# A graph-network kernel whose start is reordered: first adjacency on ScalarE's queue, late weights fetched and folded beside it

## The chip, the cores and the metric

The kernel runs on one core of one Trainium2 chip. The metric is device time in microseconds for one execution, from the first to the last instruction. Of the engines, TensorE (PE) multiplies, VectorE (DVE), ScalarE (ACT) and GpSimd (POOL) do the elementwise work, and SyncE (SP) only issues transfers. A transfer is issued in the program of one of these engines and then carried by 16 DMA engines that all queues share.

## The reference, cut to what matters

There are 16 graphs of 1024 nodes with 128 features, and each graph has a full 1024 x 1024 adjacency in float32. Two layers follow each other, each with a residual and a normalization.

```python
# layer 0: one aggregation
degree = adj.sum(axis=-1)[:, :, None]
sum_neighbors = einsum('bid,bij->bjd', x, adj) / degree
x = layernorm(x + relu(concat([x, sum_neighbors]) @ W.T + b))

# layer 1: four inner layers, which use the adjacency both ways
def _layer(nodes, adj, ws, bs, wd, bd, wn, bn, wu, bu):
    src_agg = einsum('bjv,bij->biv', nodes @ ws + bs, l2norm(adj, 2))
    dst_agg = einsum('bjv,bji->biv', nodes @ wd + bd, l2norm(adj, 1))
    upd = concat([src_agg, nodes @ wn + bn, dst_agg])
    return tanh(upd @ wu + bu)
# inner layers three and four take the outputs of earlier ones beside their own input
x = layernorm(x + layer4(layer3(layer2(layer1(x)))))
```

The product `(nodes @ ws) @ wu` is one product with folded weights `ws @ wu`. The kernel folds the weights of each inner layer once, on the chip, and keeps the folded ones in DRAM for the later graphs.

## The kernel before: the parts that the change touches

The first graph is handled apart, ahead of the loop over graphs. Transfers are issued first. The pieces of the first adjacency are split between SyncE's and GpSimd's queue; all weights and the reloaded rows of the adjacency follow on SyncE's.

```python
    def load_pair(q, pair, groups):
        h, k = pair
        for g in groups:
            q.dma_start(a[g * C:(g + 1) * C, h * BPH + k:h * BPH + k + 2], av[h][g, :, k:k + 2])
    ...
    nc.sync.dma_start(w0n, w0)
    shares = ((nc.sync, range(G // 2)), (nc.gpsimd, range(G // 2, G)))
    for h in (1, 0):
        for q, groups in shares:
            load_nodes(q, h, groups)
    make_identity(nc, ident)
    for pair in PAIRS:
        for q, groups in shares:
            load_pair(q, pair, groups)
    ...
    for l, q in enumerate((None, 2, 3, None)):
        fetched.append(fetch_weights(raw, l, nc.sync, None if l else wm))
        if q is not None:
            rows[q] = load_rows(0, q, [places[q]])
    for q in (0, 1):
        rows[q] = load_rows(0, q, [places[q]])
```

A pair is two of the eight row blocks of the adjacency. It comes in four pieces of 32 partitions and 256 KB. `fetch_weights` issues eight transfers for a layer: `ws`, `wd`, `wn`, `wu` and four biases. `load_rows` issues eight for a quarter of the adjacency's rows.

The fold of a layer has two parts. `small` takes one of two PSUM buffers in turn.

```python
    def fold_begin(l, fetched, copy=nc.scalar.copy, later=False):
        wr, wur, bc, wm, wTs = fetched
        for c in range(CHUNKS[l]):                     # CHUNKS = [1, 1, 2, 3]
            pt = small(f"wtr{l}_{c}", [BPH, P])
            for k in range(3):
                nc.tensor.transpose(pt[:, k], wr[:, k, c], ident)
            copy(wTs[c], pt[:, :3])
        pm = small(f"bm{l}", [HW])
        ...                                            # bias products into pm
        def biases():
            nc.scalar.copy(wm[:, 0], pm[:, :2 * P])
            nc.scalar.activation(bout[l], pm[:, 2 * P:2 * P + 1], AF.Identity, bias=bc[:, 3:4])
        return biases if later else biases()

    def fold_end(l, fetched):
        for c in range(CHUNKS[l]):
            pm = small(f"wm{l}_{c}", [HW])
            for k in range(3):
                nc.tensor.matmul(pm[:, k * P:(k + 1) * P], wTs[c][:, k], wur[:, PART[k]], ...)
            nc.scalar.copy(wm[:, 1 + c], pm[:, :2 * P])
            nc.scalar.copy(wown[l][:, c], pm[:, 2 * P:3 * P])
        nc.sync.dma_start(wsave[l], wm[:, :CHUNKS[l] + 1])
```

Then the first aggregation gathers the blocks pair by pair, while ScalarE squares them and VectorE sums their rows.

```python
    for h in (1, 0):
        to_xT(h)
        with_x(h)
        weights_of_x(h)
    for pair in PAIRS[:2]:
        squares_of(*pair)          # ScalarE squares, VectorE row sums
        gathers_of(*pair)          # TensorE, four products of 128 x 512
    ...
    degree_row(1)
    squares_of(*PAIRS[2])
    gathers_of(*PAIRS[2])
    ...                            # the fourth pair, the fold of layers one and two, the normalization
```

In the first inner layer the folds of layers three and four stand between the 34 products (`hooks` are run ahead of a product with that number):

```python
            hooks = {4: lambda *_: inverses(0, st0, NB), 5: folded(2, fold_begin), 6: rows0, 7: cinv0,
                     8: folded(2, fold_end), 9: lambda *_: fold_and_scale(3, 0), 11: second0, 12: folded(3, fold_end),
                     14: lambda *_: scale_rows(rows[1], 1, rinv), 18: first0, 26: sums0}
            plain_layer(b, 0, feats, t, a, at, f1, "acc", hooks)
```

The order of the instructions on TensorE, VectorE, ScalarE and GpSimd is the order in which they are written; that of SyncE's is left to the scheduler.

Of the kernel before, what the change touches and what calls it, by code (L numbers as in the profile page):

```python
# [14 lines left out]
P = 128  # L15
NL = 4
CHUNKS = [1, 1, 2, 3]
G = 4
# [5 lines left out]
def adj_resnorm_kernel(ctx: ExitStack, tc: tile.TileContext, x, adj, w0, b0, layers, out):  # L24
# [33 lines left out]
    nc = tc.nc  # L58
    B, N, D = x.shape
    NB = N // P  # L60
    HW = 512
# [9 lines left out]
    def blocks(ap):  # L71

        return ap.rearrange("p (k g c) -> p g k c", g=G, c=C)

    def nodes(ap):

        return ap.rearrange("p (g k c) -> p g k c", g=G, c=C)

    def half(h):
        return slice(h * HW, (h + 1) * HW)  # L80
# [12 lines left out]
    ident = const.tile([P, P], F32, name="ident")  # L93
    fold = const.tile([P, P], F32, name="fold")
    group = const.tile([P, G], F32, name="group")
    mhalf = const.tile([P, K], F32, name="mhalf")
    w0T = const.tile([P, 2, P], F32, name="w0T")
# [27 lines left out]
    def fetch_weights(raw, l, q, wm=None):  # L125
        ws, bs, wd, bd, wn, bn, wu, bu = layers[l]
        nch = CHUNKS[l]
        flat = raw.take(max(3 * nch * P, (nch + 1) * 2 * P))
        wr = flat[:, :3 * nch * P].rearrange("p (k c v) -> p k c v", k=3, c=nch)
        for k, w in enumerate((ws, wd, wn)):  # L130
            q.dma_start(wr[:, k], w.rearrange("(c p) v -> p c v", p=P))
        wur = raw.take(3 * P).rearrange("p (k v) -> p k v", k=3)
        q.dma_start(wur, wu.rearrange("(c p) v -> p c v", p=P))
        bc = raw.take(4)
        for k, v in enumerate((bs, bd, bn, bu)):
            q.dma_start(bc[:, k:k + 1], v.rearrange("(p o) -> p o", o=1))
        if wm is None:
            wm = flat[:, :(nch + 1) * 2 * P].rearrange("p (c v) -> p c v", c=nch + 1)
        return wr, wur, bc, wm, [raw.take(3 * P).rearrange("p (k v) -> p k v", k=3) for _ in range(nch)]
# [37 lines left out]
    def small(name, shape=(K,)):  # L177
        return ps_s.tile([P, *shape], F32, tag="small", name=name)
# [362 lines left out]
    def load_rows(b, q, st, queue=nc.sync):  # L541


        v = adj[b, q * QB * C:(q + 1) * QB * C].rearrange("(k r) (h g j) -> h g r k j", r=C, h=NH, g=G)
        n = QB // len(st)
        for i, piece in enumerate(st):
            for g in range(G):
                for h in range(NH):
                    queue.dma_start(piece[g * C:(g + 1) * C, :, h * P:(h + 1) * P], v[h, g, :, i * n:(i + 1) * n])  # L549
        return st  # L550

    def scale_rows(st, q, rinv):
        n = QB // len(st)
        for k in range(QB):
            row = st[k // n][:, k % n]
            nc.scalar.activation(row, row, AF.Copy, scale=rinv[:, q * QB + k:q * QB + k + 1])
# [248 lines left out]
    PAIRS = [(h, k) for h in (1, 0) for k in range(0, BPH, 2)]  # L805
# [5 lines that stand above are left out]
# [3 lines left out]
            q.dma_start(xn[g * C:(g + 1) * C, h * BPH:(h + 1) * BPH], xv[h][g])  # L814

    nc.sync.dma_start(w0n, w0)
    shares = ((nc.sync, range(G // 2)), (nc.gpsimd, range(G // 2, G)))
    for h in (1, 0):
        for q, groups in shares:
            load_nodes(q, h, groups)  # L820
    make_identity(nc, ident)
    for pair in PAIRS:
        for q, groups in shares:
            load_pair(q, pair, groups)
    nc.sync.dma_start(b0c, b0.rearrange("(p o) -> p o", o=1))
    raw = Raw()
    wm = message_tile("wm1_0")
    Q = combined(0, "Q")
    places = {q: Q[i].rearrange("p k (u c) -> p (k u) c", u=2) for q, i in ((2, 2), (3, 3), (0, 4))}
    places[1] = one.tile([P, 2 * NJ, HW // 2], F32, tag="T2", name="rows1_0")  # L830
    rows, fetched = {}, []
    for l, q in enumerate((None, 2, 3, None)):
        fetched.append(fetch_weights(raw, l, nc.sync, None if l else wm))
        if q is not None:
            rows[q] = load_rows(0, q, [places[q]])
    for q in (0, 1):
        rows[q] = load_rows(0, q, [places[q]])

    nc.vector.memset(mhalf, -0.5)
    nc.vector.reduce_sum(fold[:, :C], ident.rearrange("p (g c) -> p c g", g=G), axis=AX.X)  # L840
    for g in range(1, G):
        nc.vector.tensor_copy(fold[:, g * C:(g + 1) * C], fold[:, :C])
# [6 lines left out]
    def to_xT(h):  # L849
        pt = small(f"xtr0_{h}", [HW])  # L850
        for q in range(BPH):
            nc.tensor.transpose(pt[:, q * P:(q + 1) * P], xn[:, h * BPH + q], ident)
        nc.scalar.copy(nodes(xT[:, half(h)]), blocks(pt))

    pt = small("w0tr", [HW])
    for k in range(2):
        nc.tensor.transpose(pt[:, k * P:(k + 1) * P], w0n[:, k * P:(k + 1) * P], ident)
    nc.scalar.copy(w0T.rearrange("p k v -> p (k v)"), pt[:, :2 * P])

    sq = []  # L860
    for p in (3, 4):
# [73 lines left out]
    for h in (1, 0):  # L935
        to_xT(h)
        with_x(h)
        weights_of_x(h)
    for pair in PAIRS[:2]:
        squares_of(*pair)  # L940
        gathers_of(*pair)
    nc.vector.tensor_add(sq[6], sq[6], sq[7])
# [52 lines left out]
    for b in range(B):  # L995
# [8 lines left out]
        if b == 0:  # L1004
            def row_factors0():
                nonlocal rinv
                rinv = gather_inverses(0, row_inverses(0, inv))
                column_sums(0, st0)
                for q in (2, 3):
                    scale_rows(rows[q], q, rinv)  # L1010

            t = messages(b, 0, feats, wm, {0: lambda: to_x1(0), 2: row_factors0}, with_sums=False)
            cinv = {}

            def columns0(rows, h, engine=nc.vector):
                scale_columns(a, cinv[0], rows, half(h), engine)

            def rows0(destination, finish):
                for q in (2, 3):
                    transpose_rows(rows[q], q, at)  # L1020

            def cinv0(destination, finish):
                cinv[0] = factor_rows_now(0, 1, inv, "cinv")

            def second0(destination, finish):
                columns0(range(NJ, NB), 1)
                destination(1, cinv[0])
                columns0(range(NJ), 1)

            def fold_and_scale(l, q):  # L1030
                fold_begin(l, fetched[l])
                scale_rows(rows[q], q, rinv)

            def first0(destination, finish):
                columns0(range(NJ, NB), 0, nc.gpsimd)
                columns0(range(2), 0, nc.gpsimd)
                for q in (0, 1):
                    transpose_rows(rows[q], q, at)
                destination(0, cinv[0])
                columns0(range(2, NJ), 0)  # L1040

            def sums0(destination, finish):
                combine_1(y)
                finish(1)
                combine(2, y, T)
                combine_1(yt)
                combine(3, y, T)

            def folded(l, part):
                return lambda *_: part(l, fetched[l])  # L1050

            hooks = {4: lambda *_: inverses(0, st0, NB), 5: folded(2, fold_begin), 6: rows0, 7: cinv0,
                     8: folded(2, fold_end), 9: lambda *_: fold_and_scale(3, 0), 11: second0, 12: folded(3, fold_end),
                     14: lambda *_: scale_rows(rows[1], 1, rinv), 18: first0, 26: sums0}
            T = combined(0, "T")
            plain_layer(b, 0, feats, t, a, at, f1, "acc", hooks)
            wm = message_weights(b, 1)
            a2 = load(n)
            xs2 = load_spread(n)
        else:  # L1060
            w = {}
            if nxt:
                w["a"] = load(n)
                st = begin_sums(n)
            t = messages(b, 0, feats, wm)
            wm = message_weights(b, 1)
            Q = combined(b, "Q")

            def rows3():
                for q in (1, 0):  # L1070
                    transpose_rows(rows[q], q, at)

            def sums1(w=w, st=st):
                if nxt:
                    for i in range(2):
                        squares_of_row(n, w["a"], st, i)
                    for i in range(2):
                        degree_of(w["a"], st, i)

            def first_addition(st=st):  # L1080
                if nxt:
                    add_squares(n, st, 1)

            hooks = {0: rows3, 3: lambda: combine(4, y, T), 5: lambda: combine_1(yt), 7: lambda: combine(2, yt, Q),
                     9: lambda: combine(3, yt, Q), 11: lambda: combine(4, yt, Q), 17: sums1, 28: first_addition}
            aggregate(b, 0, feats, t, a, at, T, Q, f1, "row", hooks)
            a2, xs2 = w.get("a"), None
# [268 lines left out]
```

## Time and profile before

| | |
|---|---|
| time, median of 3 runs | 2435.02 us (2433.85 to 2435.8) |
| span of the profiled execution | 2438.5 us |
| TensorE's granted clock | 0.998 |
| share of DMA engines' time, SyncE's and ScalarE's kind of queue | 41.8% |
| share of DMA engines' time, GpSimd's kind of queue | 0.3% |

Times in the profile are microseconds from the first instruction. A line such as `13.33 7.11 PE L885 MATMUL pa<-a,xn ... x16` says: from 13.33 on, over 7.11 us, TensorE ran 16 records of the product at line 885, into tile `pa` from `a` and `xn`. A float32 product leaves two records. What stands in brackets is the engine's idle time before, and what ended it. `SPq` is the issuing of transfers by SyncE.

### The profile page before, as it was taken

What the parts mean: (1) busy time and instruction counts of PE and PEld (TensorE: products, weight loads), DVE (VectorE), ACT (ScalarE), POOL (GpSimd) and SP (SyncE); (2) the same over time, 40 slices, a digit from 0 to 9 for tenths busy, and PEclk for the clock granted to TensorE, in tenths of its full rate; (3) what the DMA queues carried; (4) which work ended last, traced back from release to release, by engine and by line L of the source; (5) the groups of instructions that cost most, each with busy time, mean ns of one, the idle gap of its engine ahead of it and who ended that gap; (6) DMA issues with size and microseconds to landing.
All of it is one profiled execution on the core that took longest, in us unless ns stands there. A gap on an engine that the chain in (4) does not pass through costs nothing.

```text
span 2438.5 us, 34361 instructions
## 1 busy us (share of the span) xinstructions
PE 2415.8 (99%) x13245; PEld 1058.5 (43%) x13245; DVE 1909.6 (78%) x2495; ACT 957.1 (39%) x1794; POOL 287.1 (12%) x100
## 2 busy tenths in 40 slices
PE   8999999999999999999999999999999999999998
PEld 5433444444444344443444435444443444434433
DVE  5878878798787978869788787887878878798743
ACT  5415334263342624425244351533515334262321
POOL 4101111101111011110011110111100111101100
PEclk9999999999999999999999999999999999999999
DMA  9517254261633517245172352624427254261410
GB/s 207 108 48 150 53 113 90 66 135 44 135 80 73 116 44 156 62 88 101 45 160 59 83 106 58 142 59 99 94 63 140 52 121 93 63 126 44 96 24 9
DMA packets 365732, 219.92 MB, mean 90 GB/s; under 512 B 152769, under 2 KB 336833, under 8 KB 365569
## 3 DMA queue, kind: packets, MB, share of 16 engines
q1 hardware_dynamic: 364800, 215.36, 41.8%
q0 software_dynamic: 768, 2.36, 0.3%
q8 instruction: 105, 1.72, 0.3%
q14 instruction: 59, 0.48, 0.1%
HBM read 199.17 MB, written 18.46 MB: 89 GB/s over the span
## 4 chain that ended last, share of the span: by engine, by line
PE 78%; DMA 9%; DVE 8%; SPq 2%; issue 2%; ACT 1%; DVEq 0%; ACTq 0%; POOLq 0%
PE m L773 33%; PE z L773 20%; PE pt L183 14%; PE m_f L516 5%; DMA a<-in_adj_dram 5%; PE z_f L516 2%; PE pw L183 2%; DMA rows<-in_adj_dram 2%; DVE at L564 2%; SPq L549 2%; DMA rows_acc<-in_adj_dram 1%; DVE Q L587 1%; DVE at L583 1%; DVE T L591 1%; DMA raw<-in_L_gnn_ws_dram 1%
## 5 line engine op out<-in xcount | busy, mean ns | idle before, releaser
L773 PE MATMUL m<-Q,S 128*64 128x512 f32 x1008 | 445.4, 593 | 3.1 <-DVE Q L587 2.9
L387 POOL TENSOR_TENSOR rs<-ve,mhalf 128x32 f32<-128x32 f32 x30 | 205.2, 6839 | 1955.9 <-DVE ve L385 1955.9
L773 PE MATMUL m<-at,t 128*64 128x512 f32 x1008 | 395.3, 594 | 0.3 <-DVE at L564 0.3
L773 PE MATMUL m<-T,S 128*64 128x512 f32 x1008 | 394.9, 593 | 0.0
L773 PE MATMUL m<-a,t 128*64 128x512 f32 x1008 | 392.8, 593 | 0.0
L607 DVE TENSOR_TENSOR t<-pt,wm 128x512 f32<-128x512 f32 x256 | 175.2, 689 | 159.6 <-PE pt L183 159.5
L773 PEld LDWEIGHTS m<-Q,S 128*64 128x64 f32 x1008 | 135.6, 137 | 275.2 <-issue 259.7
L773 PE MATMUL z<-Q,t 128*64 128x512 f32 x504 | 231.0, 597 | 2.0 <-DVE Q L591 2.0
L686 ACT COPY e<-m 64x512 f32<-64x512 f32 x63 | 36.6, 580 | 496.5 <-PE m L773 496.1
L773 PE MATMUL z<-a,t 128*64 128x512 f32 x504 | 231.2, 597 | 0.0
L773 PE MATMUL z<-a,S 128*64 128x512 f32 x504 | 227.1, 593 | 0.0
L773 PE MATMUL z<-at,S 128*64 128x512 f32 x504 | 226.7, 592 | 0.0
L773 PE MATMUL z<-at,t 128*64 128x512 f32 x504 | 226.6, 592 | 0.0
L183 PE MATMUL pt<-wm,f1T 128*64 128x256 f32 x1536 | 219.4, 380 | 0.0
L773 PEld LDWEIGHTS m<-T,S 128*64 128x64 f32 x1008 | 122.1, 137 | 130.1 <-issue 128.2
L773 PEld LDWEIGHTS m<-at,t 128*64 128x64 f32 x1008 | 119.8, 137 | 130.5 <-issue 127.0
L773 PEld LDWEIGHTS m<-a,t 128*64 128x64 f32 x1008 | 121.1, 137 | 122.8 <-issue 119.5
L773 PE MATMUL z<-T,t 128*64 128x512 f32 x384 | 172.8, 592 | 0.0
L345 DVE TENSOR_TENSOR a<-a,cinv 128x512 f32<-128x512 f32 x250 | 154.2, 691 | 12.8 <-DMA cinv<-dr 9.1
L183 PE MATMUL pt<-wm,f23T 128*64 128x256 f32 x1024 | 160.5, 379 | 0.0
L253 ACT ACTIVATE sq<-a 128x1024 f32<-128x1024 f32 x120 | 125.7, 1048 | 69.6 <-DVE acc L262 61.5
L183 PEld LDWEIGHTS pt<-wm,f1T 128*64 128x64 f32 x1536 | 121.7, 137 | 58.4 <-ACT f1T L786 12.0
(238 smaller groups left out, 4278.1 us busy)
## 6 DMA issues: line engine op xcount, KB each, us to landing
a<-in_adj_dram SPq DMA_DIRECT2D x120, 512.0 KB, 11.3
a<-in_adj_dram SPq DMA_DIRECT2D x240, 128.0 KB, 4.4
rows<-in_adj_dram SPq DMA_DIRECT2D x240, 64.0 KB, 3.0
wm<-wsave SPq DMA_DIRECT2D x16, 512.0 KB, 4.7
xn<-in_x_dram SPq DMA_DIRECT2D x124, 64.0 KB, 2.0
wm<-wsave SPq DMA_DIRECT2D x31, 256.0 KB, 3.7
xs<-in_x_dram SPq DMA_DIRECT2D x60, 128.0 KB, 3.6
cinv<-dr SPq DMA_DIRECT2D x30, 256.0 KB, 5.3
```

The costliest lines, as they stand in the source:

```text
L183: nc.tensor.matmul(out[s], x[:, s], y, start=start, stop=stop)
L253: nc.scalar.activation(sq, a[:, i, :], AF.Square, accum_out=state["cols"][:, i:i + 1])
L345: engine.tensor_mul(a[:, i, s], a[:, i, s], cinv[:, s])
L387: nc.gpsimd.tensor_tensor(rstd, ve, mhalf[:, :n], ALU.pow)
L516: nc.tensor.matmul(o, x_, y_, start=start, stop=stop)
L549: queue.dma_start(piece[g * C:(g + 1) * C, :, h * P:(h + 1) * P], v[h, g, :, i * n:(i + 1) * n])
L564: nc.vector.transpose(at[h][:, j:j + NJ, c].rearrange("p j (k c) -> p j k c", c=C), piece.rearrange("p k (j c) -> p j k c", c=C)[:, j:j + NJ])
L583: nc.vector.tensor_sub(y[0, 1], y[0, 1], y[0, 0])
L587: nc.vector.tensor_sub(T[2], y[1, 1], y[0, 1])
L607: nc.vector.tensor_add(t[j][:, o:o + 2].rearrange("p k a v c -> p k (a v c)"), pt, wm[:, 0][:, None, :].to_broadcast([P, 2, 2 * P]))
L686: nc.scalar.copy(e0[high], A[high])
L773: nc.tensor.matmul(o, x, y, start=start, stop=stop)
```

## The change

It rearranges the start of the first graph. The adjacency's pieces all go to ScalarE's queue; the weights of layers three and four are fetched by SyncE beside them, ahead of those of layers one and two; and these two layers are folded between the gathers of the first aggregation, so that the first inner layer is free of them. The identity is made ahead of the transfers, four products of no use are run first to raise TensorE's clock, and three copies at the start move from ScalarE to VectorE, as ScalarE is issuing then.

```diff
     nc.sync.dma_start(w0n, w0)
-    shares = ((nc.sync, range(G // 2)), (nc.gpsimd, range(G // 2, G)))
+    make_identity(nc, ident)
     for h in (1, 0):
-        for q, groups in shares:
+        for q, groups in ((nc.sync, range(G // 2)), (nc.scalar, range(G // 2, G))):
             load_nodes(q, h, groups)
-    make_identity(nc, ident)
     for pair in PAIRS:
-        for q, groups in shares:
-            load_pair(q, pair, groups)
+        load_pair(nc.scalar, pair, range(G))
+    raw = Raw()
+    fetched = {l: fetch_weights(raw, l, nc.sync) for l in (2, 3)}
     nc.sync.dma_start(b0c, b0.rearrange("(p o) -> p o", o=1))
-    raw = Raw()
     ...
-    rows, fetched = {}, []
-    for l, q in enumerate((None, 2, 3, None)):
-        fetched.append(fetch_weights(raw, l, nc.sync, None if l else wm))
-        if q is not None:
-            rows[q] = load_rows(0, q, [places[q]])
-    for q in (0, 1):
+    rows = {}
+    for l in range(2):
+        fetched[l] = fetch_weights(raw, l, nc.sync, None if l else wm)
+    for q in (2, 3, 0, 1):
         rows[q] = load_rows(0, q, [places[q]])
 
     nc.vector.memset(mhalf, -0.5)
+
+    idle = small("idle", [HW])
+    for _ in range(4):
+        nc.tensor.matmul(idle, mhalf[:, :1].to_broadcast([P, P]), mhalf[:, :1].to_broadcast([P, HW]), start=True, stop=True)
     ...
-        nc.scalar.copy(nodes(xT[:, half(h)]), blocks(pt))
+        nc.vector.tensor_copy(nodes(xT[:, half(h)]), blocks(pt))
     ...
-    nc.scalar.copy(w0T.rearrange("p k v -> p (k v)"), pt[:, :2 * P])
+    nc.vector.tensor_copy(w0T.rearrange("p k v -> p (k v)"), pt[:, :2 * P])
     ...
-    for pair in PAIRS[:2]:
+    for l, pair in zip((2, 3), PAIRS):
+        fold_begin(l, fetched[l], nc.vector.tensor_copy)
+        fold_end(l, fetched[l])
         squares_of(*pair)
         gathers_of(*pair)
     ...
-            hooks = {4: lambda *_: inverses(0, st0, NB), 5: folded(2, fold_begin), 6: rows0, 7: cinv0,
-                     8: folded(2, fold_end), 9: lambda *_: fold_and_scale(3, 0), 11: second0, 12: folded(3, fold_end),
+            hooks = {4: lambda *_: inverses(0, st0, NB), 6: rows0, 7: cinv0,
+                     9: lambda *_: scale_rows(rows[0], 0, rinv), 11: second0,
                      14: lambda *_: scale_rows(rows[1], 1, rinv), 18: first0, 26: sums0}
```

More of the change, by code (lines that the diff above doesn't have):

```diff
@@ L1028, in second0 @@
                 columns0(range(NJ), 1)
-            def fold_and_scale(l, q):
-                fold_begin(l, fetched[l])
-                scale_rows(rows[q], q, rinv)
             def first0(destination, finish):
@@ L1047, in sums0 @@
                 combine(3, y, T)
-            def folded(l, part):
-                return lambda *_: part(l, fetched[l])
-            hooks = {4: lambda *_: inverses(0, st0, NB), 5: folded(2, fold_begin), 6: rows0, 7: cinv0,
-                     8: folded(2, fold_end), 9: lambda *_: fold_and_scale(3, 0), 11: second0, 12: folded(3, fold_end),
+            hooks = {4: lambda *_: inverses(0, st0, NB), 6: rows0, 7: cinv0,
+                     9: lambda *_: scale_rows(rows[0], 0, rinv), 11: second0,
                      14: lambda *_: scale_rows(rows[1], 1, rinv), 18: first0, 26: sums0}
```

## The prediction

> **What bounds the kernel now.** I read the page first: the share of each engine, then the chain that ended last.
>
> ```profile
> PE 2415.8 (99%) x13245; PEld 1058.5 (43%) x13245; DVE 1909.6 (78%) x2495; ACT 957.1 (39%) x1794; POOL 287.1 (12%) x100
> ...
> PE 78%; DMA 9%; DVE 8%; SPq 2%; issue 2%; ACT 1%; DVEq 0%; ACTq 0%; POOLq 0%
> ```
>
> TensorE is busy for 2415.8 of 2438.5 us, so only about 22.7 us of idle exist in the whole run. Most of them must lie where the data first arrives. So I asked next for the order of time of the first 60 us (start, duration, engine, line, operation; in brackets the idle before it and what ended it).
>
> ```profile
> 3.08 4.08 SPq L810 DMA_DIRECT2D a<-in_adj_dram  x8
> 4.24 4.20 POOL L810 DMA_DIRECT2D a<-in_adj_dram  x8
> 8.14 0.35 SPq L825 DMA_DIRECT2D b0c<-in_L_gnn_b_dram  x1
> 9.26 0.35 SPq L131 DMA_DIRECT2D raw<-in_L_gnn_ws_dram  x1
> 10.82 0.33 SPq L131 DMA_DIRECT2D raw<-in_L_gnn_wd_dram  x1
> 13.31 1.06 ACT L872 ACTIVATE sq<-a 128x1024 f32<-128x1024 f32 x1 [2.19 <-DMA a<-in_adj_dram]
> 13.33 7.11 PE L885 MATMUL pa<-a,xn 128*128 128x512 f32 x16 [0.96 <-issue]
> 20.27 0.60 PE L290 MATMUL dinv<-ident,inv 128*128 128x128 f32 x4
> 42.24 1.98 PE L652 MATMUL z<-x_T,wown 128*128 128x512 f32 x4
> ```
>
> The first adjacency products start at 13.33 us, when the first pair of blocks has landed; ScalarE's square of the same block is released by that load. From there TensorE runs nearly without a gap to the aggregate of layer one (42.24). The kernel is thus bound by the first adjacency to 13.3 us and by TensorE after.
>
> SyncE's small transfers at 8.14, 9.26 and 10.82 are not spaced by their cost (0.35) but by waits. I asked for SyncE's waits up to 75 us (total, times, longest):
>
> ```profile
> SPq L136 <- DMA a<-in_adj_dram: 4.0, 3, 1.9
> SPq L131 <- DMA a<-in_adj_dram: 3.2, 3, 1.2
> ```
>
> Each transfer waits for the landing of an adjacency piece issued eight transfers earlier: the bias at 8.14 goes out as the piece of 3.08 lands (5.0 us after its issue), the next at 9.26 after the piece of 3.55 (5.4 us). The kernel has eight completion counters for these queues, handed out in turn, and at most eight transfers are out. GpSimd's queue has eight of its own, so before the change 16 adjacency pieces were out at once.
>
> The rates, from stretches of time (last two columns: DMA share, GB/s):
>
> ```profile
> 12.00:16.00 4.00, 3.04 (x8) 1.26 (x8) 2.35 (x2) 2.19 (x4) 0.41 (x1) 1.00 1.03 385
> 45.00:55.00 10.00, 9.29 (x49) 5.74 (x48) 7.37 (x11) 6.61 (x18) 1.65 (x1) 1.00 1.07 196
> 4.00:12.00 8.00, 7.54 (x18) 3.97 (x18) 0.92 (x5) 1.54 (x3) 4.55 (x10) 1.00 0.99 261
> ```
>
> Adjacency blocks in rows of 4 KB reach 385 GB/s, 261 in the mixed stretch; the reloaded rows and weights, in pieces of 512 bytes, 196 with the engines full.
>
> [...]
>
> **The change, part by part.** Its text says little of the order; the built order of the changed kernel's instructions says more.
>
> 1. *Idle products and the identity first.* The 4.3 us in which TensorE waits for the identity go, and the clock is raised early. But those products come long before the adjacency. Worth: 0.
>
> 2. *Adjacency on ScalarE's queue.* All 16 pieces are issued there, none by GpSimd. They now draw on the same eight counters as SyncE's transfers, in one merged order. Counting the merged order: w0 and x take places 1 to 9; the first pair's pieces are at places 10, 17, 23, 31; the second's at 38, 45, 50, 53; the third's at 56, 59, 62, 65; the fourth's at 68, 71, 74, 77. Between them stand the weights of all four layers and, from place 49, two row pieces (Q) for one of the adjacency. Each waits for the one eight places before it. So the last piece goes out only when place 69 has landed. And ScalarE is in order: its first table load and its first copy stand behind all 16 issues. TensorE's fold of layer three needs ScalarE to empty a PSUM buffer before its last product, and the gathers stand behind that. So the gathers start after the last issue.
>
>    When is that? Up to place 69: 13 adjacency pieces of 0.262 MB are 3.41 MB; w0 and x 0.66; layers three and four 0.59 and 0.79; one and two 0.79; 14 row pieces 1.84: 4.65 MB in small pieces. At 196 GB/s that is 23.7 us. The adjacency at some 300 (between 261 and 385, my choice) is 11.4 us. With 2 us before the first bytes: 37. I add 4 for the places where the queues, not the wires, limit: 16 transfers of layers one and two hold only 0.79 MB (4 us of wire) but at 0.43 to 0.49 us each to issue are over 7. Last issue: about 41 us.
>
>    From there: its issue 0.45, the table load 1.28, two copies of the bias product (0.37 + 0.27), one group of fold products 0.5, clock low: the gathers start at about 44, in place of 13.33. **+30.7 us.**
>
> 3. *Clock.* TensorE will have waited from about 12 to 43 us, so the first 4 us of gathers run at half speed: **+2.0 us.**
>
> 4. *Folds moved ahead.* Layer four's fold now stands between the gathers of pairs one and two, on a path that is bound by TensorE: in the trace 0.82 + 0.55 + 0.70 + 0.28 for transposes and biases, 1.50 + 0.94 for the products, 4.8 us; with waits for ScalarE, which has 1.24 us squares in between, **+6.0.** Layer three's (0.82 + 0.71 + 0.28 + 1.50 = 3.3) is hidden in the long wait.
>
> 5. *Folds taken from the first layer.* From 42.24 to 81.33 us TensorE needs 39.1 us; 34 products of two passes at 0.43 us are 29.2, the factors and sums 1.35; the folds with their waits so cost 8.5. VectorE is busy 30.9 us of that stretch, so it takes over as the limit once the stretch is some 31 to 33: I count **-6.3.**
>
> Sum: 30.7 + 2.0 + 6.0 - 6.3 = **+32.4 us**, and 2435 becomes 2467. Nothing after batch zero changes.
>
> **Rivals.** (a) *The intended gain.* If the adjacency landed as early as before (ScalarE merely taking over GpSimd's issues), the gathers would start at about 13 us, layer three's fold would be hidden, layer four's partly: -4 to -8 us, 2428 to 2431. For it: GpSimd needs 0.53 us an issue and SyncE 0.43, and a bias in SyncE's one ring took 12.7 us to land behind the adjacency. Against it: SyncE's waits show that a queue blocks at its ninth transfer, and the built order puts 61 other transfers before the last piece. (b) *Adjacency late, ScalarE not held by it.* If only the data were late, the gathers of pair one could begin after piece 31 (some 17 us) and follow the pieces; the end of the gathers would still wait for about 45 us in place of 29, +16 to +18, less the folds: 2443 to 2450. Against it: the copies stand behind the issues in ScalarE's order. (c) *Worse*: with both rings full each piece lands slower, and the last issue is at 46 or later: 2473 to 2478.
>
> **Range and chances.** The largest doubt is the last issue: 35 us if small pieces run at 230 GB/s, 46 if the adjacency gets 240. That is -6 to +5 on 2467. The clock and the gain of step 5 add 2 or 3 each way. So 2453 to 2478. A 2% loss is 2483.7: only with several of these at once. A 2% gain is out of reach, as all idle time is under 1%. Faster 0.01, same 0.93, slower 0.06.
>
> **What would show it.** In the changed profile: adjacency issues on ScalarE's queue spread to about 41 us, with waits for weights and rows (step 2); the first gather at about 44 us, right after a ScalarE copy, and TensorE idle of some 25 us ahead of it; products of the first gathers near 0.85 us apart (step 3); the weight products of layer four between the gathers (step 4); the stretch of z and d products about 33 us long (step 5). If the first gather starts before 20 us, step 2 is wrong and rival (a) holds; if gathers start near 17 and then pause for loads, (b).

## The result and the profile after

The changed kernel takes 2474.0 us at the median (2471.5 to 2474.8) against 2435.4 for the kernel before, a ratio of 1.0156 with a 95% interval of 1.0138 to 1.0173. It is slower by 38.6 us; the prediction was 2467, range 2453 to 2478.

The page of the changed kernel, busy time and the chain that ended last:

```profile
PE 2421.6 (98%) x13253; PEld 1057.7 (43%) x13253; DVE 1914.5 (77%) x2503; ACT 953.0 (39%) x1786; POOL 281.4 (11%) x88
...
PE 84%; DVE 7%; DMA 5%; ACT 1%; SPq 1%; issue 1%; DVEq 0%; ACTq 0%; POOLq 0%
```

TensorE is busy 5.8 us longer than before (2415.8), but its idle time in the span of 2473.0 has grown from 22.7 us to 51.4. The chain's shares hide that: its DMA share has even fallen, from 9 to 5%. The time is in the start, as the first 125 us in order of time show (start, duration, engine, line, operation; in brackets the idle before it and what ended it):

```profile
3.29 40.30 ACTq L810 DMA_DIRECT2D a<-in_adj_dram  x16
18.29 2.35 DVE L879 TENSOR_REDUCE cols<-a 128x1 f32<-128x1024 f32 x2 [4.53 <-DMA a<-in_adj_dram]
43.62 1.28 ACT L156 ACT_TABLE_LOAD   x1 [43.62 <-DMA Q<-in_adj_dram]
44.91 0.37 ACT L156 COPY raw<-bm 128x256 f32<-128x256 f32 x1
45.50 1.65 PE L166 MATMUL wm<-raw 128*128 128x128 f32 x6 [30.55 <-ACT bout L157]
46.95 5.56 PE L886 MATMUL pa<-a,xn 128*128 128x512 f32 x8
54.68 2.50 PE L166 MATMUL wm<-raw 128*128 128x128 f32 x18
57.02 3.60 PE L886 MATMUL pa<-a,xn 128*128 128x512 f32 x8
61.33 0.62 PE L290 MATMUL dinv<-ident,inv 128*128 128x128 f32 x4 [0.71 <-DVE inv L883]
83.32 1.98 PE L652 MATMUL z<-x_T,wown 128*128 128x512 f32 x4
114.02 1.95 PE L183 MATMUL pt<-wm,f1T 128*64 128x256 f32 x16
118.88 3.45 PE L183 MATMUL pt<-wm,f1T 128*64 128x256 f32 x16 [2.91 <-ACT f1T L786]
```

Read it from the top. ScalarE issues the adjacency from 3.29 to 43.6. VectorE sums pair one's columns at 18.29, so that pair had landed by then, 28.7 us ahead of its gathers. But ScalarE does nothing else until 43.62: its table load and the copy that TensorE's fold of layer three waits for stand behind the 16 issues in its own order. TensorE idles 30.55 us, and the gathers start at 46.95 in place of 13.33.

What the transfers did meanwhile, from stretches of time (busy time of PE, PEld, DVE, ACT, POOL; clock; DMA share; GB/s), and SyncE's waits up to 70 us (total, times, longest):

```profile
24.00:32.00 8.00, 0.00 (x0) 0.00 (x0) 0.00 (x0) 0.00 (x0) 0.00 (x0) 0.50 0.99 193
32.00:40.00 8.00, 0.00 (x0) 0.00 (x0) 0.00 (x0) 0.00 (x0) 0.00 (x0) 0.50 1.15 211
...
SPq L549 <- DMA Q<-in_adj_dram: 11.2, 16, 2.1
SPq L549 <- DMA a<-in_adj_dram: 6.2, 8, 0.9
```

For 16 us no engine computes, while the transfers run full at about 200 GB/s. SyncE's Q row pieces (one of the reloads of the adjacency's rows) wait for adjacency pieces (8 times) and for each other (16 times), and ScalarE's last wait, in the line of the table load, ended with a Q row. The two queues wait for one another's transfers. The records of the two profiled executions show the order behind it: up to 44 us, each transfer of SyncE and of ScalarE in the changed kernel signals one of the same eight semaphores (100, 102, 104 to 109), and from the ninth on each issue waits for the one that it uses itself. In the kernel before, SyncE's transfers had eight (108 to 112, 114 to 116) and GpSimd's eight others (99 to 106). These are the counters of the prediction.

### The profile page after: what moved, and what is told of

It is laid out like the page before. It is cut to its first block, busy times and chain, and to the rows that moved or that the text cites. A ratio compares the mean times of both kernels' runs of the same rounds, so it can differ in the third digit from the quotient of the medians.

```text
span 2473.0 us, 34333 instructions
## 1 busy us (share of the span) xinstructions
PE 2421.6 (98%) x13253; PEld 1057.7 (43%) x13253; DVE 1914.5 (77%) x2503; ACT 953.0 (39%) x1786; POOL 281.4 (11%) x88
## 4 chain that ended last, share of the span: by engine, by line
PE 84%; DVE 7%; DMA 5%; ACT 1%; SPq 1%; issue 1%; DVEq 0%; ACTq 0%; POOLq 0%
PE m L773 36%; PE z L773 21%; PE pt L183 15%; PE m_f L516 5%; PE z_f L516 2%; DMA a<-in_adj_dram 2%; PE pw L183 2%; DVE at L564 1%; DMA rows<-in_adj_dram 1%; SPq L549 1%; DVE acc L262 1%; DMA Q<-in_adj_dram 1%; DMA rows_acc<-in_adj_dram 1%; PE pa L886 0%; DVE at L583 0%
## 5 line engine op out<-in xcount | busy, mean ns | idle before, releaser
L345 DVE TENSOR_TENSOR a<-a,cinv 128x512 f32<-128x512 f32 x250 | 155.8, 700 | 13.2 <-DMA cinv<-dr 10.7
L183 PEld LDWEIGHTS pt<-wm,f1T 128*64 128x64 f32 x1536 | 122.3, 138 | 61.9 <-ACT f1T L786 14.9
```

What stands on the lines that cost most here:

```text
L183: nc.tensor.matmul(out[s], x[:, s], y, start=start, stop=stop)
L345: engine.tensor_mul(a[:, i, s], a[:, i, s], cinv[:, s])
```

## Experiments

Times are medians; each ratio is against the kernel before, run beside the version. Its median there lay between 2435.4 and 2438.6 us, so versions are compared by their ratios. Starts (us) are from each run's one profiled execution.

| run | first gather | dinv | time | ratio (95%) |
|---|---|---|---|---|
| before | 13.3 | 20.3 | 2435.4 | 1 |
| after | 47.0 | 61.3 | 2474.0 | 1.0156 (1.0138 to 1.0173) |
| rows_later | 26.9 | 41.3 | 2453.3 | 1.0066 (1.0050 to 1.0083) |
| copies_on_vector | 18.0 | 50.1 | 2465.0 | 1.0112 (1.0097 to 1.0127) |
| gpsimd_queue | 32.3 | 44.8 | 2457.3 | 1.0082 (1.0067 to 1.0097) |
| gpsimd_rows_later | 30.9 | 43.4 | 2455.3 | 1.0077 (1.0063 to 1.0090) |
| clock_kept | 48.5 | 61.9 | 2475.0 | 1.0153 (1.0138 to 1.0168) |
| clock_kept_longer | 49.8 | 62.2 | 2472.9 | 1.0142 (1.0128 to 1.0156) |
| no_late_folds | 12.7 | 19.6 | 2433.2 | 0.9982 (0.9974 to 0.9990) |
| shared_with_scalar | 11.6 | 21.8 | 2440.9 | 1.0010 (1.0003 to 1.0016) |
| pieces_first | 11.3 | 23.4 | 2444.6 | 1.0027 (1.0017 to 1.0038) |
| x_on_scalar | 14.0 | 21.2 | 2440.9 | 1.0017 (1.0008 to 1.0025) |
| pairs_by_queue | 14.3 | 23.0 | 2439.8 | 1.0006 (0.9997 to 1.0014) |

"dinv" is the product that makes the inverse degrees of pairs one and two; it follows both gathers and VectorE's column sums, and everything after it depends on it.

### Which transfers keep the pieces back: rows_later

The changed kernel, in which the weights of layers one and two and the rows are issued only behind ScalarE's last piece.

```diff
+            last_piece[0] = q.dma_start(a[...], av[h][g, :, k:k + 2])
-        fetched[l] = fetch_weights(raw, l, nc.sync, None if l else wm)
+        fetched[l] = fetch_weights(raw, l, behind, None if l else wm)
-        rows[q] = load_rows(0, q, [places[q]])
+        rows[q] = load_rows(0, q, [places[q]], behind)   # behind: SyncE, ordered after last_piece
```

> The changed kernel, with one edge of order added: the weights of layers one and two and the reloaded rows are issued by SyncE only behind ScalarE's last adjacency piece, so that they no longer stand among the pieces in the merged order of the eight counters. Theory (the shared counters hold ScalarE's issues back): the last piece goes out at about 17 to 18 us instead of 43.6, the gathers start at about 20.5, the factors of the degree at about 33 instead of 61.3, and the time is about 2444 us (2440 to 2450). Rival one (ScalarE's queue itself is slow, or its transfers land late whatever stands among them): the pieces still spread over some 40 us, the time stays at 2468 to 2476. Rival two (all the bytes of the start have to pass the 16 engines before the gathers end): 2460 or more.

Its order of time:

```profile
3.27 20.29 ACTq L821 DMA_DIRECT2D a<-in_adj_dram  x16
23.59 1.28 ACT L156 ACT_TABLE_LOAD   x1 [23.59 <-DMA a<-in_adj_dram]
26.91 5.52 PE L897 MATMUL pa<-a,xn 128*128 128x512 f32 x8
```

The issues end at 23.6 in place of 43.6, and the gathers come at 26.91: 20.0 us of the delay of 33.6 were the transfers of layers one and two and the rows between the pieces. The time fell to 2453.3, by more than half of the loss, and not to the expected 2444. The weights of layers three and four still stand between the pieces, and ScalarE is still held to the last one. The pieces themselves are also slower than I had taken: from 16 to 24 us ScalarE's queue has the transfer engines for itself (queue: packets, MB, share of 16 engines).

```profile
q10 hardware_dynamic: 532, 1.79, 104.2%
```

That is 223 GB/s with the engines full, where the kernel before moved 385 from 12 to 16 us. So the interleaving is a cause, and not the only one.

### Is it ScalarE's compute that waits: copies_on_vector

The changed kernel with the fold's copies of layers three and four on VectorE, so that TensorE's fold does not need ScalarE.

```diff
-    def fold_end(l, fetched):
+    def fold_end(l, fetched, copy=nc.scalar.copy):
     ...
-            nc.scalar.copy(wm[:, 1 + c], pm[:, :2 * P])
-            nc.scalar.copy(wown[l][:, c], pm[:, 2 * P:3 * P])
+            copy(wm[:, 1 + c], pm[:, :2 * P])
+            copy(wown[l][:, c], pm[:, 2 * P:3 * P])
     ...
-        fold_end(l, fetched[l])
+        fold_end(l, fetched[l], nc.vector.tensor_copy)     # and the two bias copies of these layers likewise
```

> The changed kernel, with the copies of the folds of layers three and four on VectorE instead of ScalarE; the adjacency stays late. Theory (part of the loss is that ScalarE's work stands behind its issues): the gathers of pair one start at about 18 to 19 us and those of pair two at about 29, but the factors of the degree need ScalarE's squares, which begin at about 45: factors at about 51 instead of 61.3, time about 2464 (2460 to 2468). Rival (only the lateness of the data counts, ScalarE's in-order stream does not): no change, 2472 to 2476, as the gathers would wait for their pieces anyway.

Its order of time:

```profile
17.95 5.37 PE L890 MATMUL pa<-a,xn 128*128 128x512 f32 x8 [3.10 <-DMA a<-in_adj_dram]
42.88 1.28 ACT L877 ACT_TABLE_LOAD   x1 [42.88 <-DMA Q<-in_adj_dram]
50.12 1.08 PE L294 MATMUL dinv<-ident,inv 128*128 128x128 f32 x4 [16.06 <-DVE inv L887]
```

The first gather moves from 46.95 to 17.95 and the gain is only some 9 us (11 by the ratios), as expected. ScalarE's queue still ends its issues at 42.9; its squares come after, VectorE's sums of their columns after those, and dinv stands at 50.12 behind a wait of 16 us. This is rival (b) of the prediction made real, and it is not cheap either: the squares that ScalarE owes move out behind the last issue.

### The adjacency on a queue that computes nothing: gpsimd_queue and gpsimd_rows_later

The changed kernel with all 16 pieces on GpSimd's queue; the second run also keeps the weights of layers one and two and the rows behind (as in rows_later).

```diff
-        load_pair(nc.scalar, pair, range(G))
+        load_pair(nc.gpsimd, pair, range(G))
```

> The changed kernel, with the 16 adjacency pieces on GpSimd's queue, which has eight counters of its own, instead of ScalarE's. The scheduler then also puts two row pieces ahead of the weights on SyncE. Theory (shared counters and ScalarE's blocked stream): pieces go out by their own landings, the last at 15 to 22 us, the gathers start at 15 to 17 us, the factors at about 28 to 30, time about 2440 (2436 to 2446). Rival (two rings share the engines, so adjacency beside weights is late on any queue): gathers of pair four end beyond 45 us, time 2455 or more.

> The changed kernel with the adjacency issued by GpSimd, and with the weights of layers one and two and the rows of Q, D and B put behind the weights of layers three and four, so that only those share the start with the adjacency. Theory (no queue wait holds ScalarE, but the weights get a small share of the transfer engines beside GpSimd's queue, about 70 GB/s): raw weights of layer three complete at about 12.5 us, gathers at about 15, layer four's weights at 23 to 24, dinv at about 33 instead of 61, time 2447 (2442 to 2452), still above before. Rival (only the order of issues was at fault, and the intent is sound once nothing holds ScalarE): gathers at 10 to 12 us, dinv by 22, time below 2434.

Both missed. ScalarE is free, and GpSimd's last piece is issued by 17 us in both, yet the gathers start at 32.3 and 30.9. In gpsimd_rows_later TensorE waits for weights, as its waits up to 130 us say, and the stretch from 3 to 16 us (queue: packets, MB, share of 16 engines; transfers: KB, us from issue to landing) says why:

```profile
PE wtr L147 <- DMA raw<-in_L_gnn_wn_dram: 4.0, 1, 4.0
PE wtr L147 <- DMA raw<-in_L_gnn_wd_dram: 3.8, 1, 3.8
...
q0 software_dynamic: 739, 2.46, 80.1%
q1 hardware_dynamic: 901, 0.42, 16.9%
...
raw<-in_L_gnn_ws_dram SPq DMA_DIRECT2D x1, 128.0 KB, 11.3
raw<-in_L_gnn_wd_dram SPq DMA_DIRECT2D x1, 128.0 KB, 15.0
raw<-in_L_gnn_wn_dram SPq DMA_DIRECT2D x1, 128.0 KB, 18.9
```

Here q0 is GpSimd's queue and q1 SyncE's. The two moved similar numbers of packets (739 and 901), but GpSimd's are 3.3 KB each and SyncE's 0.47 KB: six bytes on GpSimd's queue for one on SyncE's. Together they took 97.0% of the 16 engines' time. The weights of layer three, issued at 3.87, 4.35 and 4.86, land one after another at 15.2, 19.4 and 23.8 us: 131 KB in 4.3 us, 30 GB/s where I had counted on 70. By what rule the engines divide themselves between the queues is not shown. So the counters and ScalarE were not all that is wrong: fetched beside the adjacency, the weights that must be folded ahead of the gathers lose to the blocks that the gathers read.

### The clock: clock_kept and clock_kept_longer

The changed kernel with 130 and 150 idle products in layer three's fold, which keep TensorE working through the wait.

```diff
+            for _ in range(fill if c == 0 else 0):
+                nc.tensor.matmul(pm[:, 3 * P:], mhalf[:, :1].to_broadcast([P, P]), mhalf[:, :1].to_broadcast([P, P]), start=True, stop=True)
```

> The changed kernel, with 130 idle products of 128 columns put into the fold of layer three, where TensorE waits for ScalarE, so that it works from 15 to about 43 us. Theory (the clock falls during the wait, and the first gathers run at half speed): the products of pair one take 3.6 us instead of 5.56, the last fold products 0.9 instead of 1.65, time 2.0 to 2.7 us less, about 2471.5. Rival (the slow first gathers come from late data or from the weights' loads): no change beyond 0.5 us.

> As clock_kept, with 150 idle products instead of 130, so that TensorE works until about 47 us and ScalarE is free before it stops (with 130 it stopped 3.2 us early and the granted clock was back at 0.53). Theory (the clock is worth 2.0 to 2.7 us): pair one's products take 3.6 us instead of 5.56, the granted clock stays at 1.00 over the gathers, time about 2472. Rival (slow data): pair one still above 4.5 us at full clock.

The first is inconclusive: its idle products ended at 43.8, ScalarE was free at 47.0, and behind the 3.25 us of idle the granted clock was 0.55 from 47 to 48 us and 0.50 from 48 to 50 (first line). The second kept it up (the other two):

```profile
47.05 1.64 PE L166 MATMUL wm<-raw 128*128 128x128 f32 x6 [3.25 <-ACT bout L157]
3.30 43.77 ACTq L812 DMA_DIRECT2D a<-in_adj_dram  x16
49.75 3.60 PE L888 MATMUL pa<-a,xn 128*128 128x512 f32 x8
```

Pair one takes 3.60 us in place of 5.56, and the six fold products ahead 0.94 in place of 1.65: 2.7 us of the loss is the clock, of which I had counted 2.0. But in this execution the issues ran to 47.1, 3.5 us later than in the changed kernel, which hides it: 2472.9 cannot be told from 2474. The size rests on the durations and not on the time.

### What the folds are worth in the first inner layer: no_late_folds

The kernel before without the folds of layers three and four in that layer (it leaves this work out; constants stand in their place).

```diff
-            hooks = {4: lambda *_: inverses(0, st0, NB), 5: folded(2, fold_begin), 6: rows0, 7: cinv0,
-                     8: folded(2, fold_end), 9: lambda *_: fold_and_scale(3, 0), 11: second0, 12: folded(3, fold_end),
+            hooks = {4: lambda *_: inverses(0, st0, NB), 6: rows0, 7: cinv0,
+                     9: lambda *_: scale_rows(rows[0], 0, rinv), 11: second0,
```

> The kernel before, with the folds of layers three and four left out altogether (the raw weights are kept in their place, so the values are others and the work of the later graphs is the same). It measures alone what the first inner layer gains when it is free of them. Theory (VectorE takes over as the limit): the stretch of z and d products shrinks by about 8.3 us, but the next messages wait some 3 us for ScalarE's last activation, which waits for VectorE; 3.5 to 4.5 us less, about 2432. Rival (TensorE alone sets it, as step 5 counted or better): 6.3 to 8.5 us less, 2428 to 2430.

It takes 4.4 us less by the ratio (0.9974 to 0.9990) and 5.0 by the medians, about the most that taking these folds out of the layer can bring. By the prediction's count 8.5 us of folds and their waits are gone from the layer, but from the z products to the first product of the second layer 39.2 us pass in place of 44.5, 5.3 less. The rest is a wait that the kernel before does not have (first line):

```profile
77.25 1.95 PE L183 MATMUL pt<-wm,f1T 128*64 128x256 f32 x16 [3.04 <-ACT f1T L786]
PE pt L183 <- ACT f23T L786: 1.3, 1, 1.3
```

f1T is the layer's output, which VectorE's last sums feed through ScalarE. The changed kernel has the same wait, of 2.9 us. So TensorE gives up the lead in that layer to VectorE. A second new wait, of 1.3 us, follows for the next layer's output (f23T), in the changed kernel too.

### Is ScalarE a bad issuer by itself: shared_with_scalar and pieces_first

The kernel before with ScalarE in GpSimd's place for half of each pair; and with all 16 pieces on ScalarE and everything else of SyncE behind them. Both leave the folds where they were, make the identity first, run two idle products and move the three early copies to VectorE.

```diff
-    shares = ((nc.sync, range(G // 2)), (nc.gpsimd, range(G // 2, G)))
+    shares = ((nc.sync, range(G // 2)), (nc.scalar, range(G // 2, G)))
     ...
         for q, groups in shares:
-            load_pair(q, pair, groups)
+            load_pair(nc.scalar, pair, groups)     # pieces_first only
```

> The kernel before, with only this of the change: the identity first, two idle products, the three copies on VectorE, and the second half of each adjacency pair on ScalarE's queue instead of GpSimd's. The weights, rows and folds stay where they were, so nothing but adjacency stands among the first 25 places of the eight counters. Theory (the queue of ScalarE does no harm when only adjacency shares its counters): pair one lands at 9 to 10 us instead of 13, ScalarE is free at about 11, the gathers start at about 10, time 2 to 4 us less than before, about 2434. Rival (ScalarE's issues cost its squares, or eight counters in place of sixteen starve the engines): no gain or a loss, 2437 or more.

> As shared_with_scalar, but all 16 pieces on ScalarE's queue, as in the changed kernel, and the bias, weights and rows held behind the last piece in SyncE's order of issue. Theory: with nothing among the pieces, one queue with eight pieces out carries them at some 380 GB/s; the last goes out at about 12 us, the gathers start at 10 to 11, time 1 to 4 us less than before, about 2435. Rival (ScalarE's queue is slow by itself): the last piece after 18 us, time above 2440.

Both missed: by the ratios they take 2.4 and 6.6 us more than the kernel before, where 1 to 4 less were expected. In shared_with_scalar's order of time:

```profile
3.31 11.11 ACTq L810 DMA_DIRECT2D a<-in_adj_dram  x8
11.56 3.67 PE L888 MATMUL pa<-a,xn 128*128 128x512 f32 x8 [0.57 <-DMA a<-in_adj_dram]
14.51 1.28 ACT L875 ACT_TABLE_LOAD   x1 [14.51 <-DMA a<-in_adj_dram]
16.43 3.70 PE L888 MATMUL pa<-a,xn 128*128 128x512 f32 x8 [1.20 <-DMA a<-in_adj_dram]
21.75 0.62 PE L290 MATMUL dinv<-ident,inv 128*128 128x128 f32 x4 [1.62 <-DVE inv L885]
```

Pair one is there 1.8 us earlier than before, and nothing comes of it. The rest of the pieces waits: SyncE four times for an earlier piece, 6.7 us in all, so that its last piece is issued by 16.7 us in place of 7.2. Pair two is late, and ScalarE cannot start the squares before 14.5. VectorE's inverse is then late, and dinv comes at 21.75 in place of 20.27; in pieces_first at 23.40. An earlier gather is worth nothing here, as dinv waits for squares and sums.

The theory of pieces_first, one queue at some 380 GB/s, fell as well. Its stretch with nothing but adjacency under way (columns as above):

```profile
12.00:16.00 4.00, 3.09 (x8) 1.10 (x7) 1.77 (x3) 0.00 (x0) 0.00 (x0) 1.00 1.05 223
```

The engines are full and move 223 GB/s; in shared_with_scalar it is 244 in the same stretch, in the kernel before 385. So ScalarE's queue loses even when nothing stands among the pieces. Why full engines move less is open: with SyncE's and ScalarE's transfers waiting from the ninth on, at most eight pieces are out in place of up to 16, and no run parts that from the kind of queue.

### Can the start be earlier at all: x_on_scalar and pairs_by_queue

Two attempts to beat the kernel before. The first lets ScalarE issue half of x, which waits for nothing, so that GpSimd's pieces go out at 1.5 us in place of 4.24. The second gives each pair to one queue, so that pair one isn't mixed with as many other pieces. Both make the identity first and run two idle products.

```diff
-        for q, groups in shares:
+        for q, groups in ((nc.sync, range(G // 2)), (nc.scalar, range(G // 2, G))):   # x_on_scalar: x only
             load_nodes(q, h, groups)
     ...
-    for pair in PAIRS:
-        for q, groups in shares:
-            load_pair(q, pair, groups)
+    for i, pair in enumerate(PAIRS):                                # pairs_by_queue only
+        load_pair((nc.sync, nc.gpsimd)[i % 2], pair, range(G))
```

> The kernel before with two edits: the second half of x's pieces is issued by ScalarE instead of GpSimd (they wait for nothing, so ScalarE is not held and keeps its copies and an early table load), and GpSimd makes the identity first, so that its half of the adjacency goes out from about 1.3 us instead of 4.24. My theory (the start is bound by when the adjacency's pieces land, and moving transfers costs only where an engine that computes is held by its own queue): pair one lands at about 10.5 us, the gathers start at about 11 instead of 13.33, the first product of the second layer moves 1.5 to 2.5 us earlier, ratio about 0.999. Rival (the completion counters that all transfers of hardware queues share, or the wire, set when pair one lands): gathers at 12.5 to 14 us and no gain, ratio 1.000 or above.

> The kernel before with SyncE issuing the pieces of pairs one and three and GpSimd those of pairs two and four (before, each issues half of every pair), the identity made first on GpSimd and two idle products; x and everything else as before, nothing on ScalarE's queue but what it had. My theory (the transfer engines are full from the first bytes, so pair one comes earlier only if fewer pieces of other pairs are mixed with it): before, 2.4 MB of the adjacency had moved when pair one's 1.05 MB was whole; with pair one alone in SyncE's queue it should be whole after about 2.1 MB, at 11 to 11.5 us, x's products should end at 10 to 11 as the identity comes earlier, the gathers start at 11 to 11.5 instead of 13.33, and pair two be there by 15. Gain 1.5 to 2.5 us, ratio about 0.999. Rival (GpSimd's queue slows the transfers of x on SyncE's as in the run with x on ScalarE's queue, or pair two comes too late): first gather at 13 or later or a gap before pair two, no gain, ratio 1.000 to 1.002.

Neither gains; in both the rival holds. In x_on_scalar (order of time; then transfers and SyncE's waits of the first 30 us):

```profile
1.50 4.39 POOL L810 DMA_DIRECT2D a<-in_adj_dram  x8 [0.19 <-issue]
6.95 0.80 PE L855 MATMUL xtr<-ident,xn 128*128 128x128 f32 x4 [2.37 <-DMA xn<-in_x_dram]
13.98 7.22 PE L888 MATMUL pa<-a,xn 128*128 128x512 f32 x16 [0.76 <-DMA a<-in_adj_dram]
...
xn<-in_x_dram SPq DMA_DIRECT2D x4, 64.0 KB, 5.7
SPq L810 <- DMA xn<-in_x_dram: 3.3, 3, 1.3
```

Beside GpSimd's earlier pieces, x on SyncE's queue lands in 5.7 us where the kernel before has 2.7, TensorE waits for it, and the gathers come at 13.98. Waits act as well: SyncE's adjacency pieces now wait three times for x, 3.3 us in all, and the last is issued by 10.7 us in place of 7.2. The run does not part the two. In pairs_by_queue, SyncE's order of time shows its queue drain:

```profile
3.08 5.03 SPq L810 DMA_DIRECT2D a<-in_adj_dram  x8
8.15 0.42 SPq L824 DMA_DIRECT2D b0c<-in_L_gnn_b_dram  x1
10.21 0.35 SPq L131 DMA_DIRECT2D raw<-in_L_gnn_ws_dram  x1
12.39 0.33 SPq L131 DMA_DIRECT2D raw<-in_L_gnn_wd_dram  x1
14.28 0.33 SPq L131 DMA_DIRECT2D raw<-in_L_gnn_wn_dram  x1
```

Each small transfer goes out when the piece eight places before has landed: at 8.2, 10.2, 12.4, 14.3, one piece of 262 KB per 2.04 us, 128 GB/s, about half of the 252 that moved in the stretch from 8 to 12 us, which leaves 124 for GpSimd's pieces. Pair one's four pieces are complete at 14.3, and the gathers start at 14.31. Split over both queues, two of a pair's pieces land on each side at once; that is what the kernel before does, and it comes at 13.33. The whole is slower too: 287 GB/s from 12 to 16 us against 385, with as many pieces out. Here both queues go through the four groups of 32 partitions in the same order, where before SyncE's pieces were the first two groups and GpSimd's the last two; whether that is the cause no run shows. With 1.0 us more to the gathers and the clock down after the idle wait of 2.92 us (granted 0.79 from 12 to 16 us and 0.78 from 16 to 20; the first two pairs take 8.81 us, before 7.11), dinv stands at 22.96. The time, 1.0006 with an interval over 1, is not told apart from the kernel before.

No run that does all the work beats the kernel before.

## Why the prediction was right, by its steps

The time lies in the range and the mechanism is the predicted one; several terms were mis-sized. The steps below are read from the two profiles. Two readings of the kernel before were off without bearing on the sum: the second piece landed 5.7 us after its issue (5.4 is the median of two), and only 5.4 of TensorE's 22.7 us of idle lie ahead of 13.33, so not most of them.

- **Step 1, idle products and identity, worth 0.** Not isolated. In the changed kernel the idle products took 6.45 us from 0.95 on, and behind them the product of x took 1.02 us at 7.95, where the kernel before has 1.91 at 6.03. Nothing later than the gathers shows a trace of it: TensorE waits 30 us after this work.
- **Step 2, +30.7 predicted, +33.6 measured** (gathers at 46.95 against 13.33). Shown: the shared order (SyncE waits for adjacency pieces, ScalarE's last wait ends with a Q row; rows_later takes 20.0 us of it away) and ScalarE held to the last issue (copies_on_vector frees the gathers by 29 us). That waits would hold ScalarE as they hold SyncE was an estimate ahead of the result. The mis-sized term is "Last issue: about 41 us"; it was 43.6, and 42.9 to 47.1 in the profiles of the three runs that share these transfers. I had taken the adjacency at some 300 GB/s, from stretches in which two queues carried it. On ScalarE's queue alone it moved 223 (rows_later, pieces_first). At that rate, an estimate, the 3.41 MB take 15.3 us in place of 11.4, and the last issue comes at 41.0 without any allowance; of the 4 us allowed for gaps 2.6 are then left. The steps after the last issue (table load, copies, fold product) fit: 3.3 us against 3.
- **Step 3, clock, +2.0 predicted, +2.7 measured**, the 0.7 being in fold products that I had not put at low clock. No trace had shown ahead of the result how far the clock falls in a wait and how long it stays down. In the changed kernel TensorE's last product ahead of the wait ended at 14.95 us; the granted clock was 0.88 from 16 to 17 us, 0.50 from 17 to 50, 0.56 from 50 to 51 and 1.00 after that, with the products back from 45.50. clock_kept_longer takes both away.
- **Step 4, layer four's fold between the gathers, +6.0 predicted, about 5.4 measured.** From the first gather to dinv it is 14.38 us against 6.94 before, 7.4 more, of which 2.0 is the clock in pair one. The fold itself takes 4.7 (52.34 to 57.02); the waits for ScalarE that I had added do not show, but dinv waits 0.7 for VectorE's inverse.
- **Step 5, -6.3 predicted, -3.7 measured.** Here the size failed, and with it part of the reasoning. The lines behind it are, in this order, two of the kernel before, two of the changed kernel (the first a stretch of time with the clock at 0.50, columns as above), and one of clock_kept_longer:

```profile
81.26 3.89 PE L183 MATMUL pt<-wm,f1T 128*64 128x256 f32 x32
86.70 0.59 PE L773 MATMUL m<-a,t 128*64 128x512 f32 x1
120.00:121.00 1.00, 1.00 (x8) 0.63 (x6) 0.34 (x1) 0.90 (x2) 0.00 (x0) 0.50 0.00 0
124.06 0.59 PE L773 MATMUL m<-a,t 128*64 128x512 f32 x1
119.71 1.95 PE L185 MATMUL pt<-wm,f1T 128*64 128x256 f32 x16 [2.91 <-ACT f1T L788]
```

The stretch from z to the layer's last products did shrink from 39.0 to 30.7 us, more than the 6.3 I allowed. But I let the account end there. VectorE, now the later engine, delivers the layer's output through ScalarE, and the next messages take 10.0 us to the first product of the second layer against 5.4. Of these 4.6, 2.9 are the wait for f1T. Most of the rest is the clock, at 0.50 from 120 to 122 us behind that wait: the second half of the message products takes 3.45 us, the first 1.95. That loss does not always follow: after the same wait of 2.91 us in clock_kept_longer the products took 1.95, and from the z products on that execution was 1.7 us faster. no_late_folds, where the clock stayed up too, gains 5.3 in this stretch.

The terms add up to 33.6 + 2.0 + 5.4 - 3.7 = 37.3 us (the 0.7 of the fold's clock is inside the 33.6), as they must, being cut from one line of time: the first product of the second layer comes at 124.06 against 86.70, 37.4 later. The spans of the two profiled executions differ by 34.5 and the medians by 38.6; what happens behind that product stays unassigned.

**Rivals.** (a), the intended gain of 4 to 8 us, fell: the folds are worth 4.4 at most, and no queue that I tried brought the weights early without delaying something on the path. (b), data late but ScalarE not in the way, did not occur; made real in copies_on_vector, it takes 2465 and not 2443 to 2450, since I had counted only what the gathers need and not the squares. (c), the last issue at 46 or later, came up in one execution (47.1 in clock_kept_longer); the changed kernel's own was at 43.6.

What failed was my next idea, in several forms: that another order or queue would mend the start. No version gained. In the profiles, the transfer engines of the kernel before are full from 4 to 21 us (share 0.91 to 1.21 in each microsecond), and each run that brought one load forward shows another one late: x in x_on_scalar, the weights on GpSimd's queue, pair two and the squares in shared_with_scalar.

## What to carry to other kernels

Before you move transfers to an engine that also computes, list what stands behind them in its order: here ScalarE did nothing until its last issue was out at 43.6 us, held by a row on the other queue, and with fewer of that queue's transfers between its own it was free at 23.6 (rows_later). Do not count on a second queue to bring small rows early beside large ones: here it got one byte in seven (0.42 of 2.88 MB, gpsimd_rows_later). Do not take a transfer rate from a stretch with other queues than the changed kernel will have: full engines moved 385 GB/s of adjacency before and 223 on ScalarE's queue (rows_later, pieces_first). When a step is taken out of a stretch bound by one engine, follow the next engine to the point where the two meet; here 8.5 us of folds and waits less were worth 4.4.

## What the runs showed of the hardware that was not expected

- Two queues shared the transfer engines more nearly by packets than by bytes: 739 packets of 3.3 KB against 901 of 0.47 KB in the same 13 us (gpsimd_rows_later); with equal pieces on both, the one whose landings show drained at 128 GB/s (pairs_by_queue).
- Sixteen large pieces on one queue slowed another queue's small loads several times over: 128 KB of weights landed 11.3 to 19.8 us after issue beside GpSimd's pieces (both runs with that queue), and 3.3 to 3.4 us beside ScalarE's in the changed kernel, whose 16 issues were spread over 40.3 us.
- Full transfer engines moved very different amounts of the same 4 KB rows: 385 GB/s (kernel before, 12 to 16 us), 287 (pairs_by_queue), 244 (shared_with_scalar), 223 (pieces_first, and rows_later from 16 to 24 us). The cause is open.
- TensorE's clock went down behind idles of 3.25 us (clock_kept, granted 0.50 from 48 to 50 us), 2.92 (pairs_by_queue, 0.79 and 0.78 as means of 12 to 16 and 16 to 20 us) and 2.91 (changed kernel, behind f1T, 0.50 from 120 to 122 us). It did not behind idles of 2.91 (clock_kept_longer) and 3.04 us (no_late_folds): there the 16 records of the message products took 1.95 us, against 3.45 in the changed kernel. So at this length the idle alone does not decide.
